# Block products over pairs of tiles in the last stage of a three-layer kernel

## The chip, the cores and the metric

The kernel runs on one core of a Trainium2 chip. The metric is device time in microseconds: the median of three executions of the kernel before is 3495.39 us (3495.23 to 3498.11). A profile of one further execution is read beside it.

## The reference

Three layers work on x of 64 sequences of 32 rows, 512 wide (2048 rows, 16 tiles of 128 rows), in float32. The change touches only what comes after the attention of the last layer, which the code calls the tail. For every row, with y from attention, x the residual of the layer before, and s the row's sequence:

```
h      = y @ cat2                 # 128 columns of 8 experts' rank-16 factors, and 8 router logits
hw     = h[:128] * weights of the two best experts (softmax of the two top logits)
x3     = y @ W_base2 + hw @ B2 + bias2 + x
z      = x3 @ cond3[id of s]      # 32 x 32 matrices that mix the 32 rows of a sequence
out    = z @ W3 + bias3 + x3      # W3 with low-rank updates folded in beforehand
```

The two square products are y @ W_base2 (512 x 512) and z @ W3 (512 x 512).

## The kernel before

All work is float32. Layers 0 and 1 and the attention come first; the tail (class Tail, `run` from line 1591) starts when attention's pools close (`ctx.close()` and `tail.run()` at the end of attention). Its weights were loaded during attention (`weights`, line 1534): base2T and W3T as two tiles each of two 128-row chunks, cat2, B2 and two rows of bias. `fold` adds W3's updates during attention.

`run` handles one tile of 128 rows at a time, in a loop that interleaves two tiles: for T the first half (choose, base, transposes, low rank), for T - 1 the second (mixed, last). The order on TensorE is the order of the calls, since `on_pe` (line 76) chains every TensorE instruction to the one before it. The other engines' order comes from a scheduler that builds the program; DMA issues on SyncE (SP) stand in a queue in that order too. The steps, with the lines that the profile shows:

- `load`: DMA of y and x by SP (L87), a gather of the rows of cond3 by GpSimd (L1610, "sel"), and x + bias2 on GpSimd (L1613).
- `turn`: four transposes of y on TensorE (L1619) and a copy to SBUF by ScalarE (L1621, "yT").
- `choose`: the product with cat2 (PSUM "ph"), ScalarE's copy (L1629), then ten small VectorE instructions and one ScalarE exponential up to hw (L1649).
- `base`: the product with W_base2, in two parts of two chunks, 512 columns per matmul, into PSUM "po".
- `low_turn` and `low_rank`: transpose of hw (L1662), its copy (L1664), the product with B2 added into po, then on VectorE x3 = po + x (L1670) and the matrix mix (L1673), which spreads the gathered rows over a block diagonal.
- `mixed`: four products of x3 with mix into PSUM "pz", ScalarE's copy to zT (L1683), and x3 + bias3 on GpSimd (L1684).
- `last`: the product of zT with W3 (512 columns per matmul), out = po + x3 on VectorE (L1691), and the store, issued by ScalarE (L1692).

All matmuls of the tail are made in `part` and stand under L1602. The products of the attention's output with Wo stand under L931, and their sum is stored by SP at L1196 after GpSimd's adds (L1188, L1189, L1192); the tail loads what these stores wrote (y). In attention the weights of such products are already used as block sums (in_sums, out_sums).

Of the kernel before, what the change touches and what calls it, by code (L numbers as in the profile page):

```python
# [24 lines left out]
F32 = mybir.dt.float32  # L25
# [3 lines left out]
ALU = mybir.AluOpType  # L29
# [4 lines left out]
P = 128  # L34
B, S, D = 64, 32, 512
NT = B * S // P
SEQ = P // S
KC = D // P
# [1466 lines left out]
class Tail:  # L1505
# [3 lines left out]
    NE, R = 8, 16  # L1509
# [24 lines left out]
    def weights(self, x_pool, work_pool, pool, pair):  # L1534

        c, nc, a = self.c, self.c.nc, self.c.a

        def updates():
            self.A3 = x_pool.tile([P, 2, KC, P], F32, name="A3", tag="xT").rearrange("p n k f -> p n (k f)")
            self.B3 = x_pool.tile([P, 4, KC // 2, P], F32, name="B3", tag="x_sums") \  # L1540
                .rearrange("p (n a) k f -> p n (a k f)", n=2)
            for t, n in ((self.A3, "A3"), (self.B3, "B3")):
                c.load_by(t, a[n].rearrange("(k p) n -> p k n", p=P))

        def square(name):
# [4 lines left out]
            return [t[:, k, :] for t in ts for k in range(2)]  # L1550

        def last():
            self.w3 = square("W3T")
# [36 lines left out]

    def run(self):
        c, tc, nc, a = self.c, self.c.tc, self.c.nc, self.c.a
        NE, R = self.NE, self.R
        with ExitStack() as ctx:
            ip = ctx.enter_context(tc.tile_pool(name="l3_in", bufs=2, side="right"))
# [4 lines left out]
            def part(out, pairs, first, last):  # L1600
                for i, (lhsT, rhs) in enumerate(pairs):
                    c.on_pe(nc.tensor.matmul(out, lhsT, rhs, start=first and i == 0,  # L1602
                                             stop=last and i == len(pairs) - 1))

            def load(T):
                t = tiles[T]
                t["y"] = c.load(ip, "y", [P, D], self.y_in(T))
                t["x"] = c.load(ip, "x", [P, D], self.x_in(T), bufs=3)
                sel = t["sel"] = ip.tile([P, S], F32, name="sel", bufs=3)
                nc.gpsimd.indirect_dma_start(  # L1610
                    out=sel, out_offset=None, in_=a["cond3"],
                    in_offset=bass.IndirectOffsetOnAxis(ap=self.rows[:, T:T + 1], axis=0))
                nc.gpsimd.tensor_tensor(t["x"], t["x"], self.bias["bias2"], ALU.add)  # L1613

            def turn(T):
                t = tiles[T]
                pt = ps.tile([P, KC, P], F32, tag="tr", name="yT_ps")
                for k in range(KC):
                    c.on_pe(nc.tensor.transpose(pt[:, k, :], t["y"][:, k * P:(k + 1) * P], c.ident))  # L1619
                t["yT"] = ip.tile([P, KC, P], F32, name="yT")  # L1620
                nc.scalar.copy(t["yT"], pt)  # L1621

            def choose(T):

                t = tiles[T]
                ph = ps.tile([P, NE * R + NE], F32, tag="h", name="ph")
                part(ph, [(t["yT"][:, k, :], self.cat[k]) for k in range(KC)], True, True)
# [8 lines left out]
                at = ip.tile([P, 8], U32, name="at")  # L1636
# [15 lines left out]
            def base(T, u):  # L1652
                t = tiles[T]
                if u == 0:
                    t["po"] = ps.tile([P, D], F32, tag="o", bufs=2, name="po")
                part(t["po"], [(t["yT"][:, k, :], self.base[k]) for k in (2 * u, 2 * u + 1)],
                     u == 0, False)

            def low_turn(T):
                t = tiles[T]  # L1660
                pt = ps.tile([P, P], F32, tag="hw", name="hwT_ps")
                c.on_pe(nc.tensor.transpose(pt, t["hw"].rearrange("p e r -> p (e r)"), c.ident))  # L1662
                t["hwT"] = tp.tile([P, P], F32, name="hwT")
                nc.scalar.copy(t["hwT"], pt)  # L1664

            def low_rank(T):
                t = tiles[T]
                part(t["po"], [(t["hwT"], self.wB)], False, True)
                t["x3"] = tp.tile([P, D], F32, name="x3")
                nc.vector.tensor_tensor(t["x3"], t["po"], t["x"], ALU.add)  # L1670

                mix = tp.tile([P, SEQ, S], F32, name="mix")
                nc.vector.tensor_tensor(mix, t["sel"].unsqueeze(1).to_broadcast([P, SEQ, S]),  # L1673
                                        self.own.unsqueeze(2).to_broadcast([P, SEQ, S]), ALU.mult)
                t["mix"] = mix.rearrange("p j d -> p (j d)")

            def mixed(T):
                t = tiles[T]
                pz = ps.tile([P, KC, P], F32, tag="z", name="pz")
                for k in range(KC):  # L1680
                    part(pz[:, k, :], [(t["x3"][:, k * P:(k + 1) * P], t["mix"])], True, True)
                t["zT"] = tp.tile([P, KC, P], F32, name="zT")
                nc.scalar.copy(t["zT"], pz)  # L1683
                nc.gpsimd.tensor_tensor(t["x3"], t["x3"], self.bias["bias3"], ALU.add)  # L1684

            def last(T):
                t = tiles[T]
                po = ps.tile([P, D], F32, tag="o3", bufs=2, name="po3")
                part(po, [(t["zT"][:, k, :], self.w3[k]) for k in range(KC)], True, True)
                o = tp.tile([P, D], F32, name="out")  # L1690
                nc.vector.tensor_tensor(o, po, t["x3"], ALU.add)  # L1691
                nc.scalar.dma_start(self.x_out(T), o)  # L1692
                t.clear()

            load(0)
            load(1)
            turn(0)
            for T in range(NT + 1):
                if T < NT:
                    choose(T)  # L1700
                    base(T, 0)
                if T:
                    mixed(T - 1)
                if T < NT:
                    base(T, 1)
                if T + 1 < NT:
                    turn(T + 1)
                if T < NT:
                    low_turn(T)
                if T:  # L1710
                    last(T - 1)
                if T < NT:
                    low_rank(T)
                if T + 2 < NT:
                    load(T + 2)


def emit(tc, a, layers=(0, 1, 2)):
# [118 lines left out]
```

## Time and profile before

| | us |
|---|---|
| median of three runs | 3495.39 |
| the profiled execution | 3498.47 |
| its span | 3496.7 |
| first transpose of the tail starts | 3327.05 |
| first product with cat2 starts | 3328.42 |
| last DVE addition starts | 3492.88 |

Times of rows in the timeline are microseconds from the start of the span. A row names the engine (PE is TensorE, PEld its weight loads, DVE VectorE, ACT ScalarE, POOL GpSimd, SPq a DMA issue by SyncE), the line, the operation, output and inputs by the program's names, the shape and the number of instructions in it. In brackets stands the idle time before it and what ended that. The duration beside "x8" is that of the whole row of eight.

### The profile page before, as it was taken

The numbers are of one execution on the slowest core, as the hardware profiler recorded it, in microseconds if no ns is written. First come the engines' busy times: TensorE is split into PE (matmuls) and PEld (weight loads), VectorE is DVE, ScalarE is ACT, GpSimd is POOL, SyncE is SP. The second block draws the span as 40 slices with busy tenths as digits, with TensorE's granted clock in tenths as the row PEclk, the third lists the DMA queues.
The fourth block names the chain that finished last, engine by engine and source line by source line (L and its number), as shares of the span: only waits on it lengthen the run. The fifth ranks groups of instructions, "written<-read, shape, count | busy, mean of one in ns | idle before, by whom it ended". The sixth has DMA issues, their size and how long they took to land. (4 is left out here: it accounts for less than half of the span.)

```text
span 3496.7 us, 65764 instructions
## 1 busy us (share of the span) xinstructions
PE 3432.7 (98%) x20736; PEld 2601.2 (74%) x20736; DVE 2124.5 (61%) x5284; ACT 1554.7 (44%) x4089; POOL 1617.2 (46%) x1606
## 2 busy tenths in 40 slices
PE   8999999999999999999999999999999999999999
PEld 4445788888856778777787787777877778778755
DVE  4443534434457676766767767677676676766433
ACT  4111222222226555655555555555565555555411
POOL 0112432323336645645556455465564655644232
PEclk9999999999999999999999999999999999999999
DMA  6013454544466788888878888878888788887721
GB/s 220 25 34 126 159 168 154 168 151 157 139 202 213 239 261 251 259 258 256 257 249 258 255 250 258 262 251 267 256 260 262 247 267 250 259 259 241 228 85 58
DMA packets 630635, 736.00 MB, mean 210 GB/s; under 512 B 64274, under 2 KB 480018, under 8 KB 630290
## 3 DMA queue, kind: packets, MB, share of 16 engines
q1 hardware_dynamic: 577810, 558.74, 51.4%
q0 software_dynamic: 50176, 168.86, 13.9%
q8 instruction: 168, 2.75, 0.3%
q10 hardware_dynamic: 2304, 4.20, 0.3%
q14 instruction: 177, 1.45, 0.1%
HBM read 689.61 MB, written 41.94 MB: 209 GB/s over the span
## 5 line engine op out<-in xcount | busy, mean ns | idle before, releaser
L957 POOL DMA_INDIRECT vt<-in_v_rows,v_rows x512 | 512.5, 1001 | 304.9 <-PE po L931 178.7
L1220 ACT ACTIVATE pr<-pr,low 128x544 f32<-128x544 f32 x512 | 383.3, 749 | 532.3 <-DVE low L1218 486.0
L1213 PE MATMUL sc<-kt,qT 128*128 128x288 f32 (+1 forms) x2048 | 555.5, 394 | 8.1 <-DVE low L1218 6.5
L931 PE MATMUL po<-prT,vt 128*128 128x128 f32 x4096 | 544.9, 276 | 7.4 <-ACT prT L1231 5.9
L931 PEld LDWEIGHTS po<-prT,vt 128*128 128x128 f32 x4096 | 522.7, 192 | 39.1 <-ACT prT L1231 19.0
L1213 PEld LDWEIGHTS sc<-kt,qT 128*128 128x128 f32 x2048 | 385.1, 190 | 223.1 <-issue 123.0
L1218 DVE CUSTOM_DVE_ANT_0 pr<-sc,mask 128x544 f32<-128x544 f32 x512 | 368.2, 719 | 139.3 <-PE sc L1213 101.5
L1005 POOL TENSOR_TENSOR projected<-projected,swapped 128x512 f32<-128x512 f32 x160 | 208.4, 1302 | 300.9 <-DVE projected L1004 277.8
L1225 DVE TENSOR_SCALAR pr<-pr,low 128x512 f32<-128x512 f32 x512 | 315.3, 616 | 12.8
L926 PE MATMUL prT_ps<-ident,pr 128*128 128x128 f32 x2048 | 311.7, 275 | 2.6 <-DVE pr L1225 2.4
L1231 ACT COPY prT<-prT_ps 128x512 f32<-128x512 f32 x512 | 294.0, 574 | 35.2 <-PE prT_ps L926 20.1
L1222 DVE RECIPROCAL low<-low 128x1 f32<-128x1 f32 x512 | 82.0, 160 | 312.8 <-ACT pr L1220 245.7
L926 PEld LDWEIGHTS prT_ps<-ident,pr 128*128 128x128 f32 x2048 | 237.4, 142 | 11.8 <-issue 3.8
L931 PE MATMUL py<-wo,oT 128*128 128x256 f32 x1024 | 241.8, 379 | 0.0
L931 PE MATMUL pq<-wp,x_sums 128*128 128x512 f32 x512 | 240.8, 593 | 0.9 <-issue 0.5
L931 PEld LDWEIGHTS py<-wo,oT 128*128 128x128 f32 x1024 | 186.5, 190 | 21.1
L130 POOL TENSOR_TENSOR rs<-rs,minus_half 128x4 f32<-128x4 f32 x160 | 181.0, 1131 | 22.5 <-DVE low L1222 14.9
L931 PE MATMUL pq<-wp,xT 128*128 128x512 f32 x384 | 182.0, 597 | 3.9 <-DVE projected L1091 3.9
L931 PE MATMUL py<-wo,o_sum 128*128 128x256 f32 x768 | 181.4, 380 | 4.4 <-DVE o_sum L1149 2.5
L1223 ACT ACTIVATE own_pr<-pr,low 128x32 f32<-128x32 f32 x512 | 164.9, 322 | 46.2 <-DVE low L1222 37.4
L1006 POOL TENSOR_TENSOR projected<-projected,rs 128x512 f32<-128x512 f32 x160 | 172.4, 1078 | 7.9
L964 ACT COPY own_vt<-v 32x128 f32<-32x128 f32 x512 | 150.8, 295 | 54.9 <-PE po L931 42.4
(283 smaller groups left out, 6197.7 us busy)
## 6 DMA issues: line engine op xcount, KB each, us to landing
kt<-in_kT SPq DMA_DIRECT2D x2048, 64.0 KB
wp<-in_sums SPq DMA_DIRECT2D x192, 512.0 KB
wo<-out_sums SPq DMA_DIRECT2D x128, 512.0 KB
wp<-in_WqT SPq DMA_DIRECT2D x96, 512.0 KB
wo<-in_WoT SPq DMA_DIRECT2D x96, 512.0 KB
down1T<-in_down1T SPq DMA_DIRECT2D x80, 256.0 KB
wp<-in_WkT SPq DMA_DIRECT2D x32, 512.0 KB
xt<-x SPq DMA_DIRECT2D x48, 256.0 KB
```

The costliest lines, as they stand in the source:

```text
L130: self.nc.gpsimd.tensor_tensor(t, t, self.minus_half[:, :n], ALU.pow)
L926: c.on_pe(nc.tensor.transpose(pt[:, m, :], piece, c.ident))
L931: c.on_pe(nc.tensor.matmul(out, lhsT, rhs, start=first and i == 0, stop=last and i == len(pairs) - 1))
L957: nc.gpsimd.indirect_dma_start(out=vts[b % 2][:, n, :], out_offset=None, in_=a["v_rows"], in_offset=bass.IndirectOffsetOnAxis(ap=rows[h][: ...
L1005: nc.gpsimd.tensor_tensor(src, src, tmp, ALU.add)
L1006: nc.gpsimd.tensor_tensor(src, src, rs.unsqueeze(2).to_broadcast([P, REP, HD]), ALU.mult)
L1213: c.on_pe(nc.tensor.matmul(sc[:, lo + n * PSIZE:lo + m * PSIZE].rearrange("p (n k) -> p n k", k=PSIZE), q, kt[:, n:m, g, :], start=True, s ...
L1218: nc.vector.tensor_tensor_reduce(pr[:, :NK], sc[:, lo:lo + NK], masks[h, b], -SCALE, 3.0e38, ALU.add, ALU.min, low[:, 0:1])
L1220: nc.scalar.activation(pr[:, :NK], pr[:, :NK], AF.Exp, bias=low[:, 0:1], scale=-1.0, accum_out=low[:, 1:2])
L1223: nc.scalar.activation(own_prs[b % 2][:, g * S:(g + 1) * S], pr[:, L:NK], AF.Copy, scale=low[:, 2:3])
L1225: nc.vector.tensor_scalar(pr[:, :L], pr[:, :L], low[:, 2:3], None, ALU.mult)
L1231: last_prT.append(nc.scalar.copy(prT, pt).ins)
```

## The change

Only the tail changes. Two tiles form a pair (8 pairs), and the loop runs over pairs. A product of a pair with a 512 x 512 weight is taken as a product of 2 x 2 blocks: two tiles of rows, two halves of the 512 inputs, two halves of the 512 outputs. Class `Blocks` forms it by seven block products instead of eight. Each has 256 columns and two chunks of 128 inputs. They use four sums of input blocks per pair and product (`sums`, on VectorE) and four sums of weight blocks, made once (`copy_sums`, eight GpSimd instructions). The seven go into three PSUM banks as follows: p1, p6, p7, p4 accumulate one after the other in bank a; p2 in bank b; p5 and then p3 in bank c. Three partial results are taken out of PSUM on the way: after p1, p5 and p6 ScalarE copies the bank ("kept00", "kept11", "kept01"), and GpSimd adds the residual to the copy (L1659 in the new file); after p7 VectorE adds kept11 to the bank (L1676). The final additions take 256 columns each (L1686, L1687, L1689, L1691). The low-rank update of base is added to the banks in halves of 256 columns.

The first pair's base and the last pair's W3 product keep the old form (class `Plain`, 512 columns). The buffers of y go from 2 to 4, of x from 3 to 5 and of sel from 3 to 5; yT and zT hold a pair. The transposes of y and pz share one PSUM buffer (tag "tr"), and ph and the transposed hw another (tag "h").

```diff
+            def copy_sums(ws, name):
+                lo, hi = ws
+                b11, b12, b21, b22 = lo[:, :, :H], lo[:, :, H:], hi[:, :, :H], hi[:, :, H:]
+                t = fp.tile([P, 3, K2, H], F32, name=name)
+                t1, t2, t3 = (t[:, n] for n in range(3))
+                nc.gpsimd.tensor_tensor(t1, b12, b11, ALU.subtract)
+                nc.gpsimd.tensor_tensor(t3, b22, b12, ALU.subtract)
+                nc.gpsimd.tensor_tensor(t2, b22, t1, ALU.subtract)
+                t4 = fp.tile([P, K2, H], F32, name=name + "4")
+                nc.gpsimd.tensor_tensor(t4, b21, t2, ALU.subtract)
+                return {1: b11, 2: b21, 3: b22, 4: t4, 5: t1, 6: t2, 7: t3}
...
+            class Blocks:
...
+                def sums(self):
+                    x11, x12, x21, x22 = [self.xT[:, t, k * K2:(k + 1) * K2, :] for t in range(2) for k in range(2)]
+                    s = tp.tile([P, 4, K2, P], F32, name="block_sums")
+                    s1, s2, s3, s4 = [s[:, i] for i in range(4)]
+                    nc.vector.tensor_tensor(s1, x21, x22, ALU.add)
+                    nc.vector.tensor_tensor(s2, s1, x11, ALU.subtract)
+                    nc.vector.tensor_tensor(s3, x11, x21, ALU.subtract)
+                    nc.vector.tensor_tensor(s4, x12, s2, ALU.subtract)
+                    self.lhs = {1: x11, 2: x12, 3: s4, 4: x22, 5: s1, 6: s2, 7: s3}
+
+                def kept(self, src, t, u):
+                    v = tp.tile([P, H], F32, name=f"kept{t}{u}")
+                    nc.scalar.copy(v, src)
+                    nc.gpsimd.tensor_tensor(v, v, self.xs[t][:, HALF[u]], ALU.add)
+                    return v
+
+                def p(self, m):
+                    bank = {1: 0, 6: 0, 7: 0, 4: 0, 2: 1, 5: 2, 3: 2}[m]
+                    first = m in (1, 2, 5)
...
+                    part(out, [(self.lhs[m][:, k, :], self.w[m][:, k, :]) for k in range(K2)], first, True, not first)
+                    if m == 1:
+                        self.v1 = self.kept(out, 0, 0)
+                    elif m == 5:
+                        self.v5 = self.kept(out, 1, 1)
+                    elif m == 6:
+                        self.v6 = self.kept(out, 0, 1)
+                    elif m == 7:
+                        nc.vector.tensor_tensor(self.outs[1][:, HALF[1]], out, self.v5, ALU.add)
...
             def load(T):
                 t = tiles[T]
-                t["y"] = c.load(ip, "y", [P, D], self.y_in(T))
-                t["x"] = c.load(ip, "x", [P, D], self.x_in(T), bufs=3)
-                sel = t["sel"] = ip.tile([P, S], F32, name="sel", bufs=3)
+                t["y"] = c.load(ip, "y", [P, D], self.y_in(T), bufs=4)
+                t["x"] = c.load(ip, "x", [P, D], self.x_in(T), bufs=5)
+                sel = t["sel"] = ip.tile([P, S], F32, name="sel", bufs=5)
...
-            def turn(T):
+            def turn(T, tag="tr"):
...
-                pz = ps.tile([P, KC, P], F32, tag="z", name="pz")
+                pz = ps.tile([P, KC, P], F32, tag="tr", name="pz")
...
-            load(0)
-            load(1)
-            turn(0)
-            for T in range(NT + 1):
...
+            for T in range(2):
+                load(T)
+            turn(0)
+            turn(1, "h")
+            for T in range(2, 4):
+                load(T)
+            base_w = copy_sums(self.base, "base_sums")
+            w3_w = copy_sums(self.w3_pairs, "w3_sums")
+            for n in range(PAIRS + 1):
...
+                    b = bases[n] = base_of(n)
+                    b.sums()
+                    choose(2 * n)
+                    steps = iter([partial(b.p, m) for m in (1, 5, 2, 6, 3, 7, 4)] if n else
+                                 [partial(b.step, t, u) for t in range(2) for u in range(2)])
...
```

The order on TensorE within a pair n, with its second half for pair n - 1 (W3's products as w1 to w7), follows from the calls: ph of the first tile, p1, ph of the second, p5, pz of the first, p2, pz of the second, p6, p3, p7, w1, w5, p4, w2, the transposes of the next pair's first y, w6, hwT, w3, hwT, w7, the transposes of the next pair's second y, w4, and the low-rank updates.

More of the change, by code (lines that the diff above doesn't have):

```diff
@@ L1549, in square @@
                 c.load_by(t, src[:, 2 * i:2 * i + 2, :])
-            return [t[:, k, :] for t in ts for k in range(2)]
+            return ts
         def last():
-            self.w3 = square("W3T")
+            self.w3_pairs = square("W3T")
+            self.w3 = [t[:, k, :] for t in self.w3_pairs for k in range(2)]
         def low_rank():
@@ new lines, in run, with __init__, step, update @@
+            class Plain:
+                def __init__(self, tags, xT, w, updated):
+                    self.po = [ps.tile([P, D], F32, tag=tags[t], name="po") for t in range(2)]
+                    self.xT, self.w, self.updated = xT, w, updated
+                def sums(self):
+                    pass
+                def step(self, t, u):
+                    part(self.po[t], [(self.xT[:, t, k, :], self.w[k // K2][:, k % K2, :]) for k in (2 * u, 2 * u + 1)],
+                         u == 0, u == 1 and not self.updated)
+                def update(self, t, lhsT, rhs):
+                    part(self.po[t], [(lhsT, rhs)], False, True)
+                def result(self, t, out, x):
+                    nc.vector.tensor_tensor(out, self.po[t], x, ALU.add)
@@ L1664, in low_turn, with base_of @@
                 nc.scalar.copy(t["hwT"], pt)
+            def base_of(n):
+                ts = tiles[2 * n:2 * n + 2]
+                for t in ts:
+                    t["x3"] = tp.tile([P, D], F32, name="x3", bufs=4)
+                if n == 0:
+                    return Plain("ab", yTs[n], self.base, True)
+                return Blocks("abc", yTs[n], base_w, [t["x3"] for t in ts], [t["x"] for t in ts], True)
             def low_rank(T):
                 t = tiles[T]
-                part(t["po"], [(t["hwT"], self.wB)], False, True)
-                t["x3"] = tp.tile([P, D], F32, name="x3")
-                nc.vector.tensor_tensor(t["x3"], t["po"], t["x"], ALU.add)
+                bases[T // 2].update(T % 2, t["hwT"], self.wB)
+                bases[T // 2].result(T % 2, t["x3"], t["x"])
                 mix = tp.tile([P, SEQ, S], F32, name="mix")
@@ L1684, in mixed, with last_of @@
+                nc.scalar.copy(zTs[T // 2][:, T % 2], pz)
                 nc.gpsimd.tensor_tensor(t["x3"], t["x3"], self.bias["bias3"], ALU.add)
-            def last(T):
-                t = tiles[T]
[L1688 to L1692, printed above, removed]
+            def last_of(n):
+                ts = tiles[2 * n:2 * n + 2]
+                for t in ts:
+                    t["out"] = tp.tile([P, D], F32, name="out", bufs=4)
+                if n == PAIRS - 1:
+                    return Plain("de", zTs[n], self.w3_pairs, False)
+                return Blocks("def", zTs[n], w3_w, [t["out"] for t in ts], [t["x3"] for t in ts], False)
@@ L1693, in last, with stored @@
+            def stored(T):
+                t = tiles[T]
+                lasts[T // 2].result(T % 2, t["out"], t["x3"])
+                nc.scalar.dma_start(self.x_out(T), t["out"])
                 t.clear()
-            load(0)
-            load(1)
+            bases, lasts = {}, {}
+            for T in range(2):
+                load(T)
             turn(0)
-            for T in range(NT + 1):
[L1699 to L1715, printed above, removed]
+            turn(1, "h")
```

108 lines of the change are left out of this document (92 added, 16 removed).

## The prediction

> **What bounds the kernel now.** I read the page first, then the busy time by stretch, the chain that ended last, and the timeline of the tail.
>
> ```profile
> PE 3432.7 (98%) x20736; PEld 2601.2 (74%) x20736; DVE 2124.5 (61%) x5284; ACT 1554.7 (44%) x4089; POOL 1617.2 (46%) x1606
> ```
>
> ```profile
> 3400.00:3450.00 50.00, 50.00 (x195) 28.48 (x195) 19.15 (x69) 9.18 (x25) 17.21 (x15) 1.00 0.26 81
> ```
>
> The first is the page's line of busy time. The second is a stretch of the tail; its columns are window, length, then busy time of PE, PEld, DVE, ACT, POOL, the granted clock, DMA share and GB/s. PE is busy for all 50 us at clock 1.00; DVE, ACT and POOL have 60 to 80% of it free. The chain says the same:
>
> ```profile
> 3366.66 1.72 PE po L1602 x4
> 3369.27 1.72 PE po L1602 x4
> 3371.53 4.29 PE po L1602 x10
> 3376.76 1.72 PE po L1602 x4
> ```
>
> Nothing but PE is on it, and it repeats every 10.10 us (3376.76 - 3366.66), one tile. So two tiles cost 20.2 us, all of it TensorE's.
>
> **What is removed.** The price of a product is the distance between instructions, not the length of one:
>
> ```profile
> 3322.86 3.62 PE L931 MATMUL py<-wo,oT 128*128 128x256 f32 x16
> ...
> 3391.56 3.60 PE L1602 MATMUL po<-W3T,zT 128*128 128x512 f32 x8
> ```
>
> With 512 columns the last of 8 starts (3.60 - 0.59) us after the first: 7 gaps of 0.43. With 256 columns (3.62 - 0.38) / 15 = 0.216. A float32 matmul is two instructions here. Two tiles of one weight took 16 x 0.43 = 6.88 us; seven block products are 28 x 0.216 = 6.05. That is 0.83 saved, for base in pairs 1 to 7 and for W3 in pairs 0 to 6, 14 times: **-11.6 us**. The low-rank update keeps its columns (4 x 0.43 against 8 x 0.216 a pair, the same). A pair needs 20.2 - 1.66 = 18.5 us of PE.
>
> **The start.** In the built program's order the first loads of y and x have left their place among the Wo loads: they now stand behind the store of y_14 on SP, and y_1 also behind the store of y_15. Their new buffers wait for the last Wo product.
>
> ```profile
> 3297.45 0.32 SPq L87 DMA_DIRECT2D y<-y  x1
> ...
> 3324.92 3.78 SPq L1196 DMA_DIRECT2D y<-y  x2
> ...
> 3327.05 0.66 PE L1619 MATMUL yT_ps<-ident,y 128*128 128x128 f32 x4 [0.57 <-DVE y L1186]
> 3327.07 1.27 POOL L1192 TENSOR_TENSOR y<-y,y_before 128x512 f32<-128x512 f32 x1 [2.17 <-DVE y L1186]
> ...
> 3328.42 1.19 PE L1602 MATMUL ph<-cat,yT 128*128 128x136 f32 x8 [0.72 <-ACT yT L1621]
> ```
>
> Before, y_0 was issued 30 us ahead of its use. Now POOL first makes descriptors for sel (0.96, its buffer free at 3326.5), then L1192 (to about 3329.0); SP issues the store (0.33) and y_1 at about 3329.4. Loads of this size reached their user 2.8 to 3.3 us after issue (x: 3356.40 to 3359.19, 3346.31 to 3349.62). So y_1 is there at about 3332.2; turning it takes 0.6, the ScalarE copy 0.6, and both must precede the first ph: 3333.5 instead of 3328.4, +5.1, of which 0.43 (the second turn) was to be paid anyway: **+4.6**, bounds 3.5 and 6. The waits on the way through first tile and last tile were 164.4 - (16 x 10.10 - 0.43) = 3.2 us from the first ph (3328.4) to PE's end (3492.8); I count about 1.5 now (one hwT buffer used twice in pair 0, one pz buffer twice at the end): **-1.7**. The eight weight sums (8 x 1.27 on POOL) can start when the last sc has read kt, about 3297.5, and run to 3307.7; POOL was idle there but for three sel and three x adds, and the o_sum add at L1149 was held back by one of these already (1.02 instead of 0.69). I take 0, bounds -0.4 and +2.
>
> **Waits inside a pair.** No view shows these, so they are bounded. At 0 they would leave -8.7 in all. What can fill them is GpSimd:
>
> ```profile
> 3359.19 1.27 POOL L1613 TENSOR_TENSOR x<-x,bias 128x512 f32<-128x512 f32 x1 [5.97 <-DMA x<-x]
> ...
> 3359.21 1.40 DVE L1673 TENSOR_TENSOR mix<-sel,own 128x128 f32<-128x128 f32 x1 [0.29 <-PE pz L1602]
> ...
> 3460.15 0.29 DVE L1673 TENSOR_TENSOR mix<-sel,own 128x128 f32<-128x128 f32 x1 [0.28 <-PE pz L1602]
> ```
>
> The mix costs 0.29 us alone and 1.3 to 1.4 when a POOL add has just started: it ends 0.15 after that add. It reads two SBUF tensors. Adds that read one operand from PSUM do not suffer (L1091, beside POOL's adds in attention: at most 0.69 in 160). Before, POOL ran 2 x 1.27 of adds in 10.1 us, all beside free DVE time. Now it runs 4 x 1.27 + 6 x 0.73 (L1188's row) = 9.5 us of adds and two sel in 18.5, and DVE has twelve operations a pair that read two SBUF tensors: eight block sums (0.42, x_sums rows), two hw, two mix.
>
> [...]
>
> I lay out one pair from zero = DVE ends L1689 of x3 (the add that frees bank a). DVE then does L1691 and two block sums (0.35 apart, as DVE instructions overlap by 0.07), then the choice of the first tile, 1.95 us long. On POOL the first kept add runs from 2.2 to 2.95, and the x load issued at zero lands at 2.8 to 3.3, so bias2's add follows. The first holds the small e add, the second the hw product at 3.4, unless the load lands late. Then ScalarE, in order, must do d, kept11 and zT of the first tile before the second pz can use its one PSUM buffer: at 5.2 to 6.0, where PE would be there at 5.1. Next, bias3's add holds the second hw; sel waits for the mix behind it; bias3's second add meets the block sums of z. So POOL ends the third kept add at 11.9 to 12.6 (10.1 without any holding). Only that add frees the x buffer of the next odd tile (five buffers for x): its load takes 2.9, the bias2 add 1.27, the W3 kept11 add behind it 0.73, and the VectorE add that lets PE start W3's p4 0.42 more: p4 at 17.3 to 18.0 where PE's own order has it at 15.6. **Wait 1.65 to 2.35 us a pair**; I take 2.0 for pairs 1 to 5. Pairs 6 and 7 have no loads left: 1.2 (between 0.3 and 2.0). Sum 5 x 2.0 + 2 x 1.2 = **+12.4**; bounds 2 (0.3 a pair: only that L1676's 0.42 follows wp7 with 0.43 of PE work between) and 18 (POOL's chain at its longest, 2.6 a pair).
>
> **Sum.** -11.6 + 4.6 - 1.7 + 12.4 = +3.7 us. The profiled execution took 3498.47 (span 3496.7), the median is 3495.39, 3.1 lower; the difference goes on both: 3502.2 for an execution like it, 3499.1 for the median. What a measurement of this kernel can tell from no change is about 0.2%, 7 us: 3488.4 to 3502.4.
>
> **Rivals.**
> - *GpSimd becomes the bound.* From one third kept add to the next: 0.73 + load 2.9 + 1.27 + 0.73 + 0.53 to p4 of W3, 2.8 to the end of L1689, then 11.9 until the next third kept add starts (the layout above): 20.9, against 18.5 of PE; with a load of 3.3 it is 21.3. At 2.6 a pair in five and 2.0 in two, the waits are 17: +8.3, **3503.7**. It decides once the waits pass 15.7 us in all, 2.2 a pair. For it: a load stands inside POOL's order twice a pair. Against it: POOL is busy only 11.4 of 18.5 us, so any holding that DVE escapes gives slack.
> - *The holding is mostly missed.* The adds fall between DVE's, waits 0.3 to 0.5 a pair: 2 to 3.5, so -5.2 to -6.7, **3489 to 3490**; with a start 1 us shorter, 3488. For it: in the tail before, ten of sixteen mixes escaped. Against it: POOL's adds go from a quarter to a half of the time.
> - *The products aren't cheaper*: weights of 128 columns loaded (PEld 0.19) for every 0.216 of PE could pace it. The py row shows 0.216 with such loads, so this is unlikely: -11.6 becomes 0 and, with half of the waits beside the longer products, +2.9 + 6.2 = +9.1, **3504.5**.
>
> **How the numbers follow.** Forecast as summed 0.42, all within 0.2%. GpSimd bound 0.32, of which 0.30 above 3502.4. Holding missed 0.22, of which 0.12 below 3488.4 and 0.10 within. Products not cheaper 0.04, slower. So faster 0.12, same 0.54, slower 0.34. The range takes the lower bounds of waits and start (3488) and, above, the longest POOL chain with the late start (3495.4 - 11.6 + 6 - 1.7 + 18 = 3506) and 2 for the weight sums: 3488 to 3508.
>
> **What would show it.** The chain of the changed kernel should leave PE in each pair: zT or kept (ACT) before the second pz, and L1676 before p4 with POOL's kept add as its releaser. A pair should repeat every 20.5 us, not 18.5. The first ph should start 5 us later after the last Wo product than it does now. DVE's block sums should have a mean above 0.42 with single ones over 1 us, and the result adds from PSUM stay at 0.42. The groups of 256 columns should be 0.216 apart. It is wrong if the first ph is on time, if a pair takes under 19 us (then the holding is not where I put it), or if products wait on weights.

## The result, and the profile after

The changed kernel takes 3509.54 us (median of 9, 3508.90 to 3515.51); the kernel before took 3498.11 beside it (median of 9, 3495.23 to 3505.24). The ratio is 1.0033, interval 1.0023 to 1.0044: slower by 11.4 us. The forecast was 3499.1 with a range to 3508.0, so the time lies above the range, on the side of the rival "GpSimd becomes the bound" (3503.7), and beyond that too.

The profiled execution has a span of 3507.2 us, 10.5 more than that of before. The page's line of busy time, then the stretch of the tail that was shown of before (columns as there):

```profile
PE 3430.6 (98%) x20932; PEld 2637.6 (75%) x20932; DVE 2174.0 (62%) x5375; ACT 1569.4 (45%) x4131; POOL 1654.9 (47%) x1656
```

```profile
3400.00:3450.00 50.00, 45.67 (x246) 38.43 (x245) 32.81 (x87) 13.72 (x37) 28.28 (x30) 1.00 0.25 71
```

PE was busy for all 50 us of this stretch and is now idle for 4.3 of them; GpSimd's busy time went from 17.2 to 28.3, VectorE's from 19.2 to 32.8. From the first ph of one pair to that of the next it is 22.2, 21.0, 21.0, 21.0, 21.5 and 19.7 us for pairs 1 to 6, against 20.2 for two tiles before and 18.6 of PE work (the sum of the distances between starts in rows without a wait, 0.429 us for 512 columns and 0.216 for 256). The timeline of one pair shows what PE waits for:

```profile
3394.39 1.26 POOL L1701 TENSOR_TENSOR x<-x,bias 128x512 f32<-128x512 f32 x1
3394.49 1.20 DVE L1738 TENSOR_SCALAR e<-e,d 128x8 f32<-128x8 f32 x1
...
3396.58 0.59 ACT L1775 COPY zT<-pz 128x512 f32<-128x512 f32 x1
...
3397.22 1.16 PE L1606 MATMUL pz<-mix,x 128*128 128x128 f32 x8 [0.53 <-ACT zT L1775]
...
3399.80 1.10 POOL L1698 DMA_INDIRECT sel<-in_cond,rows  x1 [1.09 <-DVE mix L1764]
...
3400.32 2.17 DVE L1651 TENSOR_TENSOR block_sums<-block_sums,zT 128x256 f32<-128x256 f32 x1
...
3400.92 1.27 POOL L1776 TENSOR_TENSOR x<-x,bias 128x512 f32<-128x512 f32 x1
...
3403.34 1.13 PE L1606 MATMUL acc<-base_sums,yT 128*128 128x256 f32 x4 [0.64 <-DVE x L1676]
...
3406.89 1.26 POOL L1701 TENSOR_TENSOR x<-x,bias 128x512 f32<-128x512 f32 x1 [2.15 <-DMA x<-x]
...
3408.12 1.41 POOL L1659 TENSOR_TENSOR kept<-kept,x 128x256 f32<-128x256 f32 x2
...
3409.36 1.13 PE L1606 MATMUL acc<-w_sums,zT 128*128 128x256 f32 x4 [0.34 <-DVE out L1676]
```

There are three larger waits. The bias2 add holds an instruction of `choose` on 128x8 elements for 1.20 us (0.23 alone); d, kept11 and zT follow late on ScalarE, and so the second pz. The gather and the bias3 add hold a block sum for 2.17 us (0.42 alone); the add after p7 stands behind it in VectorE's order, and p4 of base waits for that. The bias2 add that waited for its x load delays the kept add, and p4 of W3 waits. Counted from start to start of the instructions (the brackets count from modelled ends and show less) PE loses 0.7, 0.8 and 0.5 us by them, and 0.1 more after each, where a group takes 1.13 or 1.16 us instead of 1.03 or 1.05. A small one stands in the low-rank update, which takes 1.88 us (3389.31 to 3391.19) instead of 8 x 0.216 = 1.73: its last half goes into bank b while VectorE (L1686) still reads that bank.

```profile
3390.65 0.30 PEld L1606 LDWEIGHTS acc<-B,hwT 128*128 128x128 f32 x2 [0.29 <-DVE x L1686]
```

With its 0.16 it is about 2.45 a pair.

The start, in the timeline:

```profile
3326.21 1.27 POOL L1192 TENSOR_TENSOR y<-y,y_before 128x512 f32<-128x512 f32 x1
...
3327.50 0.32 SPq L1196 DMA_DIRECT2D y<-y  x1
...
3327.86 0.43 SPq L87 DMA_DIRECT2D y<-y  x1
...
3332.09 1.12 PE L1709 MATMUL yT_ps<-ident,y 128*128 128x128 f32 x4 [3.65 <-DMA y<-y]
...
3333.88 2.18 PE L1606 MATMUL ph<-cat,yT 128*128 128x136 f32 x8 [0.68 <-issue]
```

y_1 is issued behind the store of y_15 and lands 4.2 us later; the first ph starts 12.6 us after the last row of Wo products (3321.26), not 5.6. And eight matmuls of ph take 2.18 us instead of 1.19. The busy time by stretch (last columns: granted clock, DMA share, GB/s) says why:

```profile
3329.00:3332.00 3.00, 0.00 (x0) 0.00 (x0) 0.00 (x0) 0.11 (x1) 2.39 (x3) 0.69 1.03 289
3332.00:3333.50 1.50, 1.12 (x4) 0.72 (x4) 0.29 (x1) 0.26 (x1) 1.20 (x2) 0.50 1.03 365
3333.50:3335.00 1.50, 1.12 (x5) 1.12 (x6) 0.00 (x0) 0.33 (x1) 1.35 (x2) 0.50 0.92 300
3335.00:3337.00 2.00, 2.00 (x7) 1.48 (x7) 0.53 (x4) 0.57 (x2) 1.94 (x2) 0.51 0.84 304
```

While PE waited for y_1, the granted clock fell to 0.50 and stayed there for 6.8 us ((0.31 x 3.0 + 0.5 x 1.5 + 0.5 x 1.5 + 0.49 x 2.0) / 0.5). The DMA share of 1.03 shows the loads that y_1 shared the engines with.

### The profile page after: what moved, and what is told of

The parts are those of the page before. It is cut to its first block, busy times and chain, and to the rows that moved or that the text cites. A ratio compares the mean times of both kernels' runs of the same rounds, so it can differ in the third digit from the quotient of the medians.

```text
span 3507.2 us, 66323 instructions
## 1 busy us (share of the span) xinstructions
PE 3430.6 (98%) x20932; PEld 2637.6 (75%) x20932; DVE 2174.0 (62%) x5375; ACT 1569.4 (45%) x4131; POOL 1654.9 (47%) x1656
## 5 line engine op out<-in xcount | busy, mean ns | idle before, releaser
L931 PEld LDWEIGHTS po<-prT,vt 128*128 128x128 f32 x4096 | 522.8, 192 | 37.4 <-ACT prT L1231 18.5
L1225 DVE TENSOR_SCALAR pr<-pr,low 128x512 f32<-128x512 f32 x512 | 315.2, 616 | 12.8
L1231 ACT COPY prT<-prT_ps 128x512 f32<-128x512 f32 x512 | 293.7, 574 | 35.5 <-PE prT_ps L926 18.9
L926 PEld LDWEIGHTS prT_ps<-ident,pr 128*128 128x128 f32 x2048 | 237.6, 142 | 11.6 <-issue 3.6
```

Of the source, the lines that this page charges most:

```text
L926: c.on_pe(nc.tensor.transpose(pt[:, m, :], piece, c.ident))
L1225: nc.vector.tensor_scalar(pr[:, :L], pr[:, :L], low[:, 2:3], None, ALU.mult)
L1231: last_prT.append(nc.scalar.copy(prT, pt).ins)
```

## The experiments

Theory A: inside a pair, GpSimd's adds hold VectorE's instructions on SBUF tiles, and VectorE's and ScalarE's order carries that to PE; at the start, loads behind stores and the lower clock cost the rest. Rivals: B, VectorE's own order is the bound; C, ScalarE's queue; D, the kept adds cost by being waited for; E, the order by pairs; F, what the start gains is waited for elsewhere.

Since the part before the tail varied between profiles (the last row of Wo products starts at 3320.7 to 3331.8 us, with no order that follows the edits; the profiles of e2, e3, e4, e11 and e12, for one, have a stretch of 3.4 us at a granted clock of 0.50 between 3279 and 3289 us, after a wait of 1.9 us, which those of the kernel before and the changed one lack), the table also gives the tail alone, from that row to the end of the span, and the length of the pairs 2 to 4, from the same profiles. "Against before" is the median less that of the kernel before on the same chip; the ratio is the record's own and not that of the medians (for e3 and e4 it gives 15 us where the medians give 18.5 and 17.0).

| | against before, us | ratio (interval) | first ph after the row, us | pairs 2 to 4, us | tail, us |
|---|---|---|---|---|---|
| before | | | 5.6 | 20.2 | 173.8 |
| changed | +11.4 | 1.0033 (1.0023 to 1.0044) | 12.6 | 21.0 | 185.9 |
| e1_loads_first | +10.3 | 1.0030 (1.0020 to 1.0040) | 6.1 | 20.9 to 21.0 | 181.3 |
| e2_kept_vector | +27.1 | 1.0073 (1.0059 to 1.0087) | 12.4 | 23.8 to 23.9 | 201.5 |
| e3_pz_two | +18.5 | 1.0043 (1.0029 to 1.0057) | 13.0 | 20.6 to 21.0 | 189.2 |
| e4_x_eight | +17.0 | 1.0042 (1.0028 to 1.0056) | 12.7 | 20.5 to 21.3 | 187.5 |
| e5_adds_vector | -0.4 | 0.9996 (0.9987 to 1.0005) | 12.4 | 19.1 to 19.2 | 173.9 |
| e6_bias_vector | +2.6 | 1.0007 (0.9999 to 1.0016) | 12.5 | 19.7 | 176.9 |
| e7_plain_pairs | +10.9 | 1.0030 (1.0019 to 1.0041) | 12.5 | 20.8 | 185.4 |
| e8_combined | -7.4 | 0.9983 (0.9972 to 0.9993) | 6.1 | 19.1 | 164.2 |
| e9_unread_adds | +19.0 | 1.0056 (1.0043 to 1.0069) | 12.8 | 21.4 | 193.7 |
| e10_start_only | +8.4 | 1.0023 (1.0014 to 1.0032) | 6.1 | 20.9 to 21.0 | 180.3 |
| e11_kept_sbuf | +5.6 | 1.0014 (1.0005 to 1.0023) | 12.9 | 20.0 to 20.3 | 181.7 |
| e12_combined2 | -6.9 | 0.9978 (0.9969 to 0.9987) | 6.2 | 18.9 to 19.0 | 163.9 |

### The loads first

```diff
+            lp = ctx.enter_context(tc.tile_pool(name="l3_load", bufs=1, side="right"))
             fp = ctx.enter_context(tc.tile_pool(name="l3_sums", bufs=1, side="right"))
...
-                t["y"] = c.load(ip, "y", [P, D], self.y_in(T), bufs=4)
+                t["y"] = c.load(lp, "y", [P, D], self.y_in(T), bufs=3)
```

and x and sel from lp too.

> Edit: y, x and sel of the tail get a pool of their own that is allocated first (y with 3 buffers instead of 4), so that their first loads need not wait for the last Wo product; the sums of weight blocks take the place behind it. In the changed kernel the first ph starts 12.6 us after the last row of Wo products (5.6 in the kernel before), and the first 3.1 us of the tail run at a granted clock of 0.50. Theory A (the start is lost to loads that stand behind the stores of y_14 and y_15, and the idle time brings the lower clock): first ph 6.0 to 6.5 us after that row, clock 1.00 throughout, 7 to 8 us less than the changed kernel, near 3502. Rival B (the first pair is held by GpSimd: the weight sums now stand between the first tiles' adds and are late for p5 of pair 1): under 4 us gained, 3506 or more, with a wait at p5 of pair 1. The waits inside pairs 1 to 7 stay as they are in both (period 21.0 us).

The first ph is back (6.1 us) and no stretch of low clock lies there, but only 4.6 us of the tail are gained, 1.1 of the time: in size that is rival B, though its wait stands in the first pair and not at p5 of the next. GpSimd now makes the weight sums (each 1.27) while VectorE chooses for the first tiles:

```profile
3337.71 1.26 POOL L1618 TENSOR_TENSOR w_sums<-W3T,w_sums 128x512 f32<-128x512 f32 x1
3337.81 1.19 DVE L1739 TENSOR_SCALAR e<-e,d 128x8 f32<-128x8 f32 x1
...
3343.02 0.30 PE L1747 MATMUL hwT_ps<-ident,hw 128*128 128x128 f32 x1 [2.11 <-DVE hw L1741]
```

The second hw is 2.11 us late for its transpose, and the first pair takes 14.0 us. Pair 5 takes 23.9 instead of 21.5: two block sums in a row are held (2.20 and 1.62), p4 of base waits 2.07 us, and the clock is 0.50 for the 3.4 us after it. And before the tail PE waits 1.9 and 3.1 us at the two places where the changed kernel waits 0.6 and 2.2. So what costs inside a pair can cost at the start too, by the same pair of engines.

### Kept adds straight from PSUM

```diff
-                    nc.scalar.copy(v, src)
-                    nc.gpsimd.tensor_tensor(v, v, self.xs[t][:, HALF[u]], ALU.add)
+                    nc.vector.tensor_tensor(v, src, self.xs[t][:, HALF[u]], ALU.add)
```

> Edit: the residual is added to p1, p5 and p6 by VectorE straight from PSUM, one instruction in place of ScalarE's copy and GpSimd's add. In the changed kernel a pair takes 21.0 us, of which 2.3 are PE's waits: 0.8 before the second pz, 0.9 before p4 of base, 0.6 before p4 of W3. Theory A (GpSimd's adds hold VectorE and its order delays the adds behind the x load): the wait before p4 of W3 goes, that before the second pz falls by ScalarE's copy (0.35), that before p4 of base stays since the bias3 add and not a kept add holds the block sums; period 20.0, about 6 us less, near 3503. Rival B (VectorE becomes the bound: 6 x 0.42 more of it, and the add after p6 must come before p7): a new wait at p7, period 21 or more, 3509 to 3515. Rival C (ScalarE's queue is the cause and GpSimd is not): the second pz alone gains, 0.35 a pair, 3507.

Rival B was right here, and too small: 27 us over before. Bank a must be read between p6 and p7, and the reader now stands in VectorE's order:

```profile
3391.51 2.17 DVE L1652 TENSOR_TENSOR block_sums<-zT 128x256 f32<-128x256 f32 x1
3392.11 1.27 POOL L1775 TENSOR_TENSOR x<-x,bias 128x512 f32<-128x512 f32 x1
...
3393.93 0.41 DVE L1658 TENSOR_TENSOR kept<-acc,x 128x256 f32<-128x256 f32 x1
...
3394.39 0.94 PE L1606 MATMUL acc<-base_sums,block_sums 128*128 128x256 f32 x2 [2.35 <-DVE kept L1658]
```

The hold by the bias3 add now reaches p7 through it. The lower clock comes with this wait as well: after it in pairs 2 to 5 (2.35 to 2.81 us), and after one of 2.05 us in pair 1, the granted clock is 0.50 for 3.4 us (the four matmuls of p7 last 1.78 to 1.80 us instead of 1.03). It is again the hold, one instruction further down the order, so this run alone doesn't tell A from B.

### Two buffers for pz

```diff
-                pz = ps.tile([P, KC, P], F32, tag="tr", name="pz")
+                pz = ps.tile([P, KC, P], F32, tag="h" if T % 2 else "tr", name="pz")
```

> Edit: pz of the second tile of a pair goes into the other shared PSUM buffer (tag h), so it need not wait until ScalarE has copied zT of the first. Theory A (the hold on VectorE by GpSimd sets p4 of base whatever comes before it): the wait of 0.8 us before the second pz goes, and the wait before p4 of base grows by about as much; period 20.7 to 21.0, 0 to 2 us less, 3508 to 3509.5. Rival C (ScalarE's queue, in which d, kept11 and zT stand in order, is what costs the time): period 20.2, 5 to 6 us less, near 3504.

As A had it: the wait at the second pz is gone, and p4 of base waits 0.8 longer (0.64 before the same instruction in the changed kernel):

```profile
3394.35 1.13 PE L1606 MATMUL acc<-base_sums,yT 128*128 128x256 f32 x4 [1.43 <-DVE x L1676]
```

Pairs 2 and 3 stay at 21.0. In two pairs this wait is 2.01 and 2.10 us, and a stretch of lower clock follows (the next group of W3 takes 1.91 us instead of 1.03; the pairs take 23.8 and 23.2 us). The time is 7 us over the changed kernel's by the medians. In the profiles, where it is 12.1, 3.3 lie in the tail and the rest before it, where the edit changes nothing that I can name. C falls.

### Eight buffers for x

```diff
-                t["x"] = c.load(ip, "x", [P, D], self.x_in(T), bufs=5)
+                t["x"] = c.load(ip, "x", [P, D], self.x_in(T), bufs=8)
```

> Edit: eight buffers for x instead of five, so that no x load waits for the third kept add of the running pair. Theory A (the x load of the odd tile stands in GpSimd's order ahead of the kept add that p4 of W3 waits for): the wait of 0.6 us before p4 of W3 goes in pairs 1 to 5, about 2.5 us less, near 3507; the waits before the second pz and before p4 of base stay or move by where the bias2 adds then fall. Rival B (the wait before p4 of W3 comes from the last ScalarE copy and VectorE add, which the buffers don't touch): within 1 us of 3509.5.

The four pairs 2 to 5 take 1.4 us less together (20.84, 21.31, 20.48, 20.54 against 21.00, 21.02, 21.03, 21.48), not 2.5: in pair 3 the wait before p4 of W3 stays (0.8), and where it falls to 0.3, in pairs 4 and 5, that before p4 of base grows from 0.63 to 1.02. The chain through the x load is a small part of it. The time says nothing for either side: 1.6 us more in the tail (start and first pairs), the rest before it.

### All adds on VectorE, and the bias adds alone

```diff
-                    nc.gpsimd.tensor_tensor(v, v, self.xs[t][:, HALF[u]], ALU.add)
+                    nc.vector.tensor_tensor(v, v, self.xs[t][:, HALF[u]], ALU.add)
...
-                nc.gpsimd.tensor_tensor(t["x"], t["x"], self.bias["bias2"], ALU.add)
+                nc.vector.tensor_tensor(t["x"], t["x"], self.bias["bias2"], ALU.add)
...
-                nc.gpsimd.tensor_tensor(t["x3"], t["x3"], self.bias["bias3"], ALU.add)
+                nc.vector.tensor_tensor(t["x3"], t["x3"], self.bias["bias3"], ALU.add)
```

> Edit: all ten adds per pair that GpSimd made in the changed kernel (bias2, bias3, the residual onto p1, p5 and p6) are made by VectorE, on the same tiles; GpSimd keeps the gathers and the weight sums. Theory A (what costs the time inside a pair is that VectorE and GpSimd hold each other up: each VectorE instruction on SBUF tiles that meets a GpSimd add takes 1.2 us instead of 0.2 to 0.4): VectorE has about 5.2 us more work a pair and still less to wait for; the waits of 2.3 us a pair fall to 0 to 0.6, period 18.8 to 19.3, 10 to 14 us less than the changed kernel, near 3497. Rival B (VectorE's order is the bound: whatever moves to it is late for p7 or p4, as the adds of e2 were): period 20.5 or more, 3506 or more.

A: the pairs take 19.1 to 19.2 us, all six of them, and the tail is 12.0 us shorter. VectorE has 36.5 busy us in the stretch where it had 32.8, and PE 49.8:

```profile
3400.00:3450.00 50.00, 49.76 (x280) 43.15 (x279) 36.51 (x134) 15.72 (x43) 2.98 (x3) 1.00 0.24 75
```

Its timeline, at the place of the holds:

```profile
3391.33 0.16 DVE L1737 TENSOR_TENSOR e<-e 128x8 f32<-128x8 f32 x1
...
3391.52 0.23 DVE L1738 TENSOR_SCALAR e<-e,d 128x8 f32<-128x8 f32 x1
...
3396.42 0.42 DVE L1651 TENSOR_TENSOR block_sums<-block_sums,zT 128x256 f32<-128x256 f32 x1
```

From the second pair on, L1737 took 0.15 to 0.16 here in all 14, and 0.57 to 1.19 in all 14 of the changed kernel. With five microseconds more of its own work a pair, VectorE is no bound: B falls.

The last two of these edits without the first:

> Edit: only the bias2 and bias3 adds (four a pair, 1.27 us each) go from GpSimd to VectorE; the six adds onto kept tiles (0.73 each) stay on GpSimd. Theory A (the long adds hold VectorE, and the bias2 add stands between the x load and the kept add): period 19.2 to 20.0, 5 to 10 us less than the changed kernel, and a wait before p4 of W3 of at most 0.4. Rival D (the six new adds are what holds it): period within 0.5 of 21.0.

19.7 us a pair, and 9.0 us less of tail: A. The four long adds are worth 1.3 us a pair alone.

### The order by pairs with the old products

```diff
-                if n == 0:
+                if True:
                     return Plain("ab", yTs[n], self.base, True)
```

and the same for W3; the steps of Plain everywhere, no weight sums.

> Edit: every product of the tail in the old form (512 columns, eight block products' worth), in the new order by pairs; so no block sums, no kept tiles and no weight sums. Bias adds stay on GpSimd. Theory A (the waits come with the kept tiles and block sums, not with the order by pairs): PE needs 20.2 us a pair and gets them, period 20.2 to 20.5; with the late start (12.6 us to the first ph, and the lower clock there) about 9 us over the kernel before, near 3507. Rival E (the order by pairs itself brings the waits, by the one pz buffer and ScalarE's queue): period 21 or more, 3513 or more.

+10.9 us with no block product at all, as much as with fourteen. The pairs take 20.8, between A's 20.5 and E's 21: in this form no product is left between the two transposes of hw, which share a buffer, and the second waits 0.41 us. So the products did save what they should, and their waits took it back: 185.4 and 185.9 us of tail.

### Adds that nobody reads

```diff
                 nc.scalar.copy(zTs[T // 2][:, T % 2], pz)
+                nc.gpsimd.tensor_tensor(self.unread, zTs[T // 2][:, T % 2].rearrange("p k f -> p (k f)"),
+                                        self.bias["bias3"], ALU.add)
```

on top of e5, and one like it with yT and bias2 after each turn.

> Edit: e5 (all adds on VectorE, period 19.13 us) and on top of it four adds of 128x512 a pair on GpSimd whose result nobody reads: one after each turn, of yT and bias2, one after each zT, of zT and bias3. Nothing waits for them but the next gathers, which are pairs ahead of their use. Theory A (an add on GpSimd holds VectorE while it runs, whoever reads it): VectorE's small instructions grow to over 1 us beside them, PE waits, period 19.6 to 21, 3 to 12 us over e5, 3502 to 3511. Rival D (the adds cost by being waited for, in the order on GpSimd): period 19.1 to 19.2, as e5, 3499.

19.1 became 21.4 us a pair by adds whose result is never used:

```profile
3404.32 1.75 POOL L1779 TENSOR_TENSOR unread<-zT,bias 128x512 f32<-128x512 f32 x1 [6.66 <-ACT zT L1778]
3404.84 1.25 DVE L1740 TENSOR_TENSOR e<-e 128x8 f32<-128x8 f32 x1
...
3407.28 1.90 DVE L1651 TENSOR_TENSOR block_sums<-zT 128x256 f32<-128x256 f32 x1
3407.61 1.27 POOL L1779 TENSOR_TENSOR unread<-zT,bias 128x512 f32<-128x512 f32 x1
...
3409.23 1.13 PE L1607 MATMUL acc<-w_sums,block_sums 128*128 128x256 f32 x4 [0.39 <-DVE block_sums L1651]
```

This is the cleanest of the runs: nothing waits for the add, yet VectorE stands still beside it. D falls. The tail is 20 us longer than in e5, but 5.8 of that lie in the first pair, where one mix (L1767, 0.28 us alone) took 8.86 us from 3334.11 on: it stood beside seven GpSimd adds in a row, six of them sums of weight blocks. What the unread adds cost by themselves is the 2.2 us a pair.

### The kept adds alone

The first of the three edits of e5 without the others.

> Edit: only the six adds onto kept tiles (0.73 us each on GpSimd) go to VectorE, after ScalarE's copy as in e5; the bias adds (1.27 us each) stay on GpSimd. e6 moved the other four: 21.0 to 19.7 a pair. Theory A (the long adds hold VectorE at the second pz and at p4 of base; the kept adds cost only at p4 of W3): the wait of 0.6 there goes, the two others stay or grow by the 0.42 that VectorE has more: period 20.3 to 21.3, 0 to 5 us less than the changed kernel. Rival D (the kept adds hold it as much): period 19.2 to 20, 7 to 12 us less.

20.0 to 20.3 us a pair: 0.7 to 1.0 less, at the edge between the two expectations. The six short adds hold VectorE as well, by less: moved alone 0.8, and on top of the long ones 0.6 (19.7 to 19.1). Together with the 1.3 of e6 this gives 2.1 of the 1.9 that e5 gained: for these 1.9 us no other cause is needed. Of the 0.6 that PE still waits in a pair of e5, 0.24 stand before p4 of W3, where L1676 follows p7, and 0.16 in the low-rank update.

### The start alone

e1, with the weight sums in the buffers of attention's values:

```diff
+        tail.spare = vts
         tail.run()
...
-                t = fp.tile([P, 3, K2, H], F32, name=name)
-                t1, t2, t3 = (t[:, n] for n in range(3))
+                t1, t2, t3, t4 = (spare[:, n, :].rearrange("p (k h) -> p k h", k=K2) for n in range(4))
```

> Edit: the changed kernel with the loads' own pool of e1, and the weight sums in the buffers of attention's values (free before the tail), so that neither the loads nor the sums are in the first pair's way; adds on GpSimd as in the changed kernel. Theory A: first ph 6.0 us after the last row of Wo products instead of 12.6, clock 1.00 there, first pair 12.6 instead of 14.1, and pairs 1 to 5 unchanged at 21.0 to 22.2: 7 to 8 us less than the changed kernel, near 3502. Rival F (what the start gains is waited for in pair 1 or at the end of attention, as in e1): 3506 or more.

First ph 6.1 us, first pair 12.6, no lower clock there: the start is as A had it. Still only 5.6 us of tail and 3 of time. What the tail lacks is in pair 5, as in e1; what the time lacks beyond that lies before the tail, which is F. Pair 5 takes 23.9 instead of 21.5: p4 of base waits 2.1 us, since two block sums in a row are held (2.21 and 1.62), and then the clock falls. And at the end of attention PE waits twice for 1.9 us where the changed kernel waits 0.6 and not at all: in the second of them GpSimd's bias2 adds, whose x now lands early, and VectorE's o_sum adds hold each other up (3.92 us for two of the one, 3.42 for two of the other). The first has no cause that I can show.

### Together

e10 with two pz buffers and all adds on VectorE, but for the first five bias2 adds:

> Edit: the loads' own pool of e1; the weight sums written into the buffers of attention's values, which are free earlier; pz of the second tile in the other buffer as in e3; residual and bias adds on VectorE as in e5, but the first five bias2 adds on GpSimd. Theory A: the start is back (first ph 6.0 us after the last row of Wo products, 8 us less), pairs of 18.7 to 19.2 us (13 us less): 3487 to 3490, faster than the kernel before by 8 to 11 us. Rival B (VectorE's order): pairs of 20 and more, 3495 to 3500.

A for the tail (164.2 us, 9.6 less than before the change); 7.4 us of it reach the time, a little under the 8 to 11 expected. The end of attention keeps its two waits of 1.9 us, as in e10. The last run goes after the second:

```diff
-                t["y"] = c.load(lp, "y", [P, D], self.y_in(T), bufs=3)
+                t["y"] = lp.tile([P, D], F32, name="y", bufs=3)
+                c.load_by(t["y"], self.y_in(T))
...
-            w3_w = copy_sums(self.w3_pairs, self.spare[1])
+            w3_w = copy_sums(self.w3_pairs, fp.tile([P, 4, D], F32, name="w3_sums"), nc.vector)
```

> Edit: e8, and the loads of y and x ordered behind the loads of the Wo weights, and the sums of W3's blocks on VectorE in a pool of their own behind the last Wo product. In e8 the products of o_sum waited 1.9 us more than in the kernel before, beside GpSimd adds (bias2 of the first tiles, W3's sums) that met VectorE's o_sum adds. Theory A: that wait goes, 1.5 to 3 us less than e8: 3489 to 3490.5, 8 to 10 us under the kernel before. Rival F (the loads then land late or the sums on VectorE delay the first choice): 3491 to 3495.

The second wait is gone, the first (1.94 us, before the last head's po) is not. The pairs take 18.9 us, 0.3 above PE's own 18.6. The time is no better than that of e8: the profiled execution has a granted clock of 0.50 for 10 us, from the first of the two waits at the end of attention (1.94 and 2.10 us) on, which that of e8 lacks. Six of the twelve executions have a mean granted clock of 0.994 to 0.996 and take 3496.6 to 3500.3 us, the profiled one among them; the other six have 0.997 or 0.998 and take 3486.7 to 3491.6. So the median of e12 lies between two groups that the clock sets apart. By their intervals, e8 and e12 both beat both kernels; which of them is better these runs don't tell.

## Why the prediction was wrong

The sum was +3.7 us; the profiles show +10.5. Its terms, in order:

| term | predicted | measured |
|---|---|---|
| block products | -11.6 | -11.4 |
| start | +4.6 (3.5 to 6) | +8.2 |
| edges (waits in the first and the last tile) | -1.7 | -1.2 |
| weight sums, end of attention | 0 (-0.4 to +2) | -1.6 |
| waits in pairs 1 to 7 | +12.4 (2 to 18) | +16.4 |
| sum | +3.7 | +10.4 |

Two steps failed: the start, outside its bounds, by the price of the load and by the clock; and the waits in a pair, whose path was another one than the sum followed.

- **Products.** Right: the groups of four matmuls last 1.03 us, so (1.03 - 0.38) / 3 = 0.217 apart. The low-rank update keeps its price too: its eight halves take 1.73 us in pair 7, and in pairs 1 to 5 of e12. The 1.88 of the other pairs is a wait for VectorE's reading of bank b and is counted with the waits.
- **Start.** This step failed. The order of the issues was right to 0.1 us (y_1 was expected 6.5 us after the last row of Wo products and came at 6.6). But its load was priced at the 2.8 to 3.3 of single x loads, and took 4.2 among others. And the clock had no term: a wait of 3.65 us for the load halved it for 6.8 us, of which 4.9 fell on PE work: 0.5 on the turn and 1.6 on ph and the first products. The whole is 7.06 - 0.43 (the second turn) + 1.6.
- **Waits in a pair.** The cause was right, VectorE held beside GpSimd's adds (e5 and e9). The path was not. The 2.0 us a pair came from one chain: third kept add, x load, bias2 add, kept add, p4 of W3. PE loses 0.5 us there. The larger losses are 0.7 at the second pz, which the layout had on the way, and 0.8 at p4 of base, which it did not have: the add after p7 stands behind the block sums in VectorE's order. That 2.0 came near the measured 2.45 of pairs 2 to 4 is in good part luck (it is 3.6 in the first pair, 2.9 in pair 5). What is held was only partly right as well. The prediction named what "reads two SBUF tensors", block sums, hw and mix, and of the small instructions of choose the e add. But no mix met an add here (0.28 or 0.29 in all 16) and hw did in two of 16 (0.87), while of choose the instructions with one tensor and a scalar were held too (L1736, 0.63 to 0.70 instead of 0.21; L1738, up to 1.24 instead of 0.23). The bias3 adds, which the layout has meet the block sums, took 1.26 to 1.29 us in the changed kernel, all 16 of them.
- **The rival that came closest** gave 20.9 to 21.3 a pair by a chain of kept add, x load, bias2 add and kept add on GpSimd. The pair takes 21.0, but not for that reason: e4 takes the load out of the chain and gains a third of a microsecond a pair, and e9 reaches 21.4 with no chain at all.
- **The signs** named ahead: adds from PSUM stay at 0.41 to 0.43, eleven of them beside a GpSimd add (right); block sums have a mean of 0.58 with five of 2.16 to 2.20 (right); the spacing of 256 columns (right); 20.5 a pair (21.0) and 5 us to the first ph (7.1) were too low.
- **The end of attention.** The row of -1.6 is not shown to come from the weight sums. The last products of attention's values start 2.9 us earlier than before, but 1.3 of that are there at 3150 us already, and the rest comes as the profile of before has waits of 1.9 us at 3216 and 3279 that this one lacks and e1's has; then the o_sum products run 1.3 us longer, some 3.4 us of them at a clock of 0.50 after a wait of 2.2 us. In the profile of before, a wait of 2.5 us at this place brought no such stretch. Whether it comes is, by these rows, not a matter of the wait's length alone.

The terms add up to 10.4, the 10.5 within rounding. The median of before was 3495.39 when the prediction was made and 3498.11 over nine runs, so the 3.1 us that were taken off for it should not have been. That alone moved the forecast time and its range down by about 2.7 us: as a difference, the range ended at +12.6, and the measured +11.4 lies inside it. The prediction also gave 1.02 us to the o_sum add that was held before the change; that is the distance to the next start, and the add itself took 1.10.

## What to carry to other kernels

The work moved to an idle GpSimd was not free here, where VectorE works on SBUF tiles on the critical path: beside the adds, VectorE's instructions of 0.15 to 0.42 us took up to 2.20. Count what VectorE loses beside each add, not whether GpSimd has room; in e5 VectorE made the same adds in about half the time (0.68 us instead of 1.27 for a bias add, 0.42 instead of 0.73 for a kept one), and PE's waits in a pair went from 2.45 to 0.6 us. Trace each hold to the next instruction in the same engine's order that PE needs, since that is where it is paid. And price a new wait of TensorE with the clock after it, not only with itself: with the 3.65 us at the start the clock was 0.50 for 6.8 us, with 2.2 us at the end of attention for 3.4, and with 2.5 us there in the kernel before it stayed at 1.00.

## What the runs showed of the hardware

- Beside a GpSimd add, VectorE instructions of 0.15 to 0.42 us took up to 1.24 (L1737 and L1738) or 2.20 us (block sums); a cast of 128x8 elements took 4.10 us in the first pair (0.17 in the other 15), while four bias2 adds ran from 3336.01 to 3340.93. Adds with one operand in PSUM took 0.41 to 0.43 beside them. Like that cast, a mix was held through a whole run of adds in e9: it took 8.86 us beside seven in a row. GpSimd lost little in the pairs of the changed kernel, where its kept adds took 0.72 to 0.96; in e9 an unread add took 1.75 instead of 1.27 (at 3404.32). At the end of attention in e10 both sides lost: adds of 1.27 took 1.71 to 1.96 beside VectorE's long o_sum adds. MAX8 and RECIPROCAL, with one input, stayed at 0.15 to 0.17 beside adds (L1723 and L1732, changed kernel).
- The block sums of 2.17 began beside a gather, which two others had passed at 0.42, and were held through its last half microsecond and the whole add behind it, in five of five. In e5, where no add follows the gathers in the pairs, nothing beside them took longer than it does alone. The other way round it happened once: a gather took 3.25 us instead of 0.95 to 1.02 (e12, from 3358.20 on) beside nine VectorE instructions in a row, eight of them with two SBUF inputs.
- The granted clock fell to 0.50 after waits of TensorE of 2.2 us (end of attention, changed kernel) and 2.35 us (p7 in e2), for 3.4 us (3.41 in the profiles of both kernels) or two or three times that (6.83 us at the start of the changed kernel's tail, some 10 us at the end of attention in e12), and not after 2.5 us in the kernel before. A wait of 1.89 us (e12, to 3281.48) had such a stretch behind it, and one of 1.90 us at the same place in the kernel before (to 3278.82) had none.
